# Two layers with attention, scan and experts: the experts' slots emptied in pieces, from zeros in memory, during the second batch

## The chip, the cores and the metric

The kernel runs on one core of a Trainium2 chip. The metric is device time in microseconds (us), as the median of several runs of the whole program. The core has five engines with a queue each: TensorE (PE, with its weight loads PEld), VectorE (DVE), ScalarE (ACT), GpSimd (POOL) and SyncE (SP). SP does nothing but issue transfers. POOL issues transfers too, the gathering and scattering ones among them. All transfers are carried out by 16 DMA engines.

## The reference

There are two layers over x of shape (4, 1024, 256), in float32. Each adds the product of a branch and a gate to x:

```python
xn = _layernorm(x)
s = attention_and_mlp(xn)            # layer 0: linear attention with cos and sin features
g = silu(rwkv_ffn(xn))
x = x + s * g
xn = _layernorm(x)
s = mamba(xn)                        # layer 1: a scan over time with 16 states
g = silu(two_experts(xn))            # layer 1: routed experts, this part is touched
x = x + s * g
```

The experts are routed. For every token a softmax over 8 experts is taken and the best two are picked. The first one works on the token; the second one works on the token plus half of the first one's output. The two outputs are weighted by their gate values, added to the token and normalised:

```python
topk_vals, topk_idx = top_k(softmax(x @ gate_W + gate_b), 2)
eo0 = expert[topk_idx[0]](x)
eo1 = expert[topk_idx[1]](x + 0.5 * eo0)
out = layernorm(x + topk_vals[0] * eo0 + topk_vals[1] * eo1)
```

## The kernel before, in words

The 4096 tokens are taken in 8 blocks of 512 (TB), two to a batch. Layer 0 goes batch by batch. For each batch there are eight key groups and eight query groups (the loop over `groups` in the kernel's main part). In one group, PE projects keys or queries (L729, L740), ACT and DVE take the sines (L762, L764, L765, L397), and PE multiplies them into kv or pa (L801, L832). Around these groups other work is dealt out in small steps from generators: `before_attention` (normalisation L506 to L522, transposes, projections), `after_attention` (the MLP with its weights fetched by L630 and L637, the second branch), and, as soon as a block is through layer 0, the scan of layer 1 (`decay` with the bcs load L946 on SP, `scan_step` with L1014, L1017 or L1023, L1032 and L1035).

When all blocks are through layer 0, the experts run beside the rest of the scan. Tokens are sorted by their expert through a table in memory. `slots[0]` has 5888 rows (NPAD, that is 23 tiles of 256) of 260 words for the first choice; `slots[1]` has rows of 516 words for the second choice. GpSimd scatters the tokens into their slots (L1272) and reads each tile of slots back with a plain transfer (L1291). Not every slot gets a token. An empty slot has to hold zeros and, in its last four words, row numbers that lie beyond the used part, so that what is computed for it is scattered where nobody reads. So the first 5888 rows of both tables are emptied before the scatters. The zeros come from `blank` and the four last words from `nowhere`, which is filled by POOL (L1125, L1127). The scatters are made to wait for the emptying through the lists `blanked`.

What sets the order of the work: the whole program is first written down in program order. At the end `arrange` replays it with assumed durations and one assumed queue for all transfers, and picks for PE, DVE and ACT one instruction after another: among those that are ready, the one with the lowest turn. A turn is the place in program order, moved for some names by a number of instructions (the table LATER). The order found is then fixed for these three engines. The queues of SP and POOL are not fixed by it.

```python
SIGNAL, LANDING, PER_BYTE = 60.0, 2000.0, 1 / 260
ENGINES = ("PE", "DVE", "Activation")
...
x.turn = k + LATER[behind].get(x.engine, {}).get(re.sub(r"_?[ab]?\d.*$", "", name), 0)
...
queue = max(queue, free[engine] + 300) + x.bytes * PER_BYTE
end = queue + LANDING - 300
```

On-chip tiles of one tag share a fixed number of buffers. `blank` is such a tile of the tag "w" in the pool work0, with five buffers, which also holds the x blocks of layer 0.

Of the kernel before, what the change touches and what calls it, by code (L numbers as in the profile page):

```python
# [15 lines left out]
F32 = mybir.dt.float32  # L16
U32 = mybir.dt.uint32
# [6 lines left out]
P = 128  # L24
# [17 lines left out]
ROW = 2 * D + 4  # L42
# [322 lines left out]
def kernel(  # L365
# [3 lines left out]
    nc = tc.nc  # L369
    const = ctx.enter_context(tc.tile_pool(name="const", bufs=1))  # L370
    dram = ctx.enter_context(tc.tile_pool(name="dram", bufs=1, space=DRAM))
# [17 lines left out]
    def col(name, i=0):  # L389
        return vec[:, COL[name] + i : COL[name] + i + 1]  # L390
# [10 lines left out]
    def accumulate(ps, pairs):  # L401
        for i, (lhs, rhs) in enumerate(pairs):
            nc.tensor.matmul(ps, lhs, rhs, start=i == 0, stop=i == len(pairs) - 1)  # L403
# [10 lines left out]
    def bank(name):  # L414
        return ps_bank.tile([P, TB], F32, name=name, tag="bank")
# [5 lines left out]
    work = l0.enter_context(tc.tile_pool(name="work0", bufs=5))  # L421

    def fetch_x(j):
        t = work.tile([P, NT, D], F32, name=f"x_{j}_{nc.next_id()}", tag="w")
        nc.gpsimd.dma_start(out=t, in_=tokens(x[j * TB : (j + 1) * TB, :]))
        return t
# [8 lines left out]
        out=bias_s, in_=rows_a.rearrange("a d -> (a d)").partition_broadcast(P)  # L435
# [62 lines left out]
    def normalize(pool, src, tag, twice=False):  # L498


        st = small.tile([P, NT, 6], F32, name=f"st_{tag}", tag="ln_st")
        bufs = 4 if twice else 2
        mv = pool.tile([P, NT, 2], F32, name=f"mv_{tag}", tag="ln_mv", bufs=bufs)
        rs = pool.tile([P, NT], F32, name=f"rs_{tag}", tag="ln_rs", bufs=bufs)
        for t in range(NT):
            nc.vector.bn_stats(st[:, t, :], src[:, t, :])  # L506
            nc.vector.bn_aggr(mv[:, t, :], st[:, t, :])
        nc.vector.tensor_scalar(rs, mv[:, :, 1], EPS, None, ALU.add)
        nc.gpsimd.tensor_tensor(rs, rs, mhalf, ALU.pow)
        if not twice:  # L510
            return mv, rs
        both = small.tile([P, NT], F32, name=f"rs2_{tag}", tag="ln_rs2")
        nc.vector.tensor_tensor(both, rs, rs, ALU.mult)
        nc.vector.tensor_tensor(both, both, mv[:, :, 1], ALU.mult)
        nc.vector.tensor_scalar(both, both, EPS, None, ALU.add)
        nc.gpsimd.tensor_tensor(both, both, mhalf, ALU.pow)
        nc.vector.tensor_tensor(both, both, rs, ALU.mult)
        return mv, rs, both

    def apply(dst, src, mv, rs):  # L520
        for t in range(NT):
            nc.vector.tensor_scalar(  # L522
                dst[:, t, :], src[:, t, :], mv[:, t, 0:1], rs[:, t : t + 1], ALU.subtract, ALU.mult
            )

    def transposed(src, c, tag):

        ps = bank(f"tr_{tag}")
        for t in range(NT):
            nc.tensor.transpose(ps[:, t * P : (t + 1) * P], src[:, t, c * P : (c + 1) * P], ident)  # L530
        return ps
# [4 lines left out]
    def bias(n, tiles=NT):  # L536

        return bias_s[:, n : n + 1, :].to_broadcast([P, tiles, D])

    def before_attention(b, s):  # L540

        j = b * (L // TB) + s
        tag = f"a{j}"
        xi = x_first if j == 0 else fetch_x(j)
        yield "N"
        mv, rs, both = normalize(keep, xi, tag, twice=True)
        kept[j] = (mv, rs)
        apply(xi, xi, mv, both)
        yield "N"
        x2t = work.tile([P, NC, TB], F32, name=f"x2t_{tag}", tag="w")  # L550
        for c in range(NC):
            ps = transposed(xi, c, f"{tag}{c}")
            nc.scalar.activation(
                x2t[:, c, :], ps, AF.Identity, bias=col("ln1_b", c), scale=col("ln1_g", c)
            )
        yield "N"
        qt = keep.tile([P, NC, TB], F32, name=f"qt_{tag}", tag="qt", bufs=2)
        kt = keep.tile([P, NC, TB], F32, name=f"kt_{tag}", tag="kt")

        v = keep.tile([P, NT, D + DH], F32, name=f"v_{tag}", tag="v")  # L560
        for dst, w, name in ((qt, wq_s, "bq"), (kt, wk_s, "bk")):
            for m in range(NC):
                ps = bank(f"p{name}_{tag}{m}")
                accumulate(ps, [(w[:, c, m * P : (m + 1) * P], x2t[:, c, :]) for c in range(NC)])
                nc.scalar.activation(dst[:, m, :], ps, AF.Identity, bias=col(name, m))
            if name == "bq":
                yield "K"
        nc.gpsimd.memset(v[:, :, D:], 0.0)
        for i in range(NT // 2):
            ps = bank(f"pv_{tag}{i}").rearrange("p (u d) -> p u d", u=2)  # L570
            for u in range(2):
                t = 2 * i + u
                accumulate(
                    ps[:, u, :],
                    [(x2t[:, c, t * P : (t + 1) * P], wv_s[:, c, :]) for c in range(NC)],
                )
            nc.vector.tensor_tensor(v[:, 2 * i : 2 * i + 2, :D], ps, bias(0, 2), ALU.add)
        keys[b, s] = (qt, kt, v)
# [513 lines left out]
    def beside(j, hf):  # L1092
# [23 lines left out]
    NPAD = NST * TS  # L1116
    slots = [
        dram.tile([NPAD, ROW - D], F32, name="slots0", tag="slots0"),
        dram.tile([2 * NPAD, ROW], F32, name="slots1", tag="slots1"),
    ]  # L1120
    fused = dram.tile([NB * L + NPAD, D], F32, name="fused", tag="fused")
    blank = work.tile([P, ROW - 4], F32, name="blank", tag="w")
    nc.gpsimd.memset(blank, 0.0)
    nowhere = w1p.tile([P, NPAD // P, 4], U32, name="nowhere", tag="nowhere")
    nc.gpsimd.memset(nowhere, 0)  # L1125
    for at_col, first in ((0, NPAD), (2, NB * L)):
# [1 line left out]
            nowhere[:, :, at_col], pattern=[[P, NPAD // P]], base=first, channel_multiplier=1  # L1128
        )
    blanked = ([], [])  # L1130
    for k, t in enumerate(slots):
        a = t[:NPAD, :].rearrange("(a p) d -> p a d", p=P)
        width = a.shape[2] - 4
        blanked[k].append(
            nc.sync.dma_start(
                out=a[:, :, :width],
                in_=blank[:, :width].unsqueeze(1).to_broadcast([P, NPAD // P, width]),
            )
        )
        blanked[k].append(nc.sync.dma_start(out=a[:, :, width:].bitcast(U32), in_=nowhere))  # L1140

    def needs(later, earlier):
        tc.add_manual_dep(
# [379 lines left out]
    def first_unit():  # L1523
        yield from prepare_block(0)
        yield from prepare_unit(0, 0)

    before.add(before_attention(0, 0))
    while before.force():
        pass
    for b in range(NB):  # L1530
        groups = [("k", b, s, t) for s in range(2) for t in range(NT)]
        groups += [("q", b, s, m, par) for s in range(2) for m in range(NC) for par in range(2)]
        for c, group in enumerate(groups):
            if c == 0:
                before.add(before_attention(b, 1))
            elif c == 4:
                while before.force():
                    pass
            elif c == 12 and b + 1 < NB:
                before.add(before_attention(b + 1, 0))  # L1540
            if before.wants == "K" and c >= 12:
                before.wants = "N"
            cycle(group, quota=(2, 3 if scans.ahead else 6, 2 if scans.ahead else 6, 0))
            for s in range(2):
                if len(at.get((b, s), ())) == NC:
                    after.add(after_attention(b, s, at.pop((b, s))))
            if 0 in ready and not blocks and not scans.side.todo:
                scans.side.add(first_unit())
                while not units:
                    scans.side.force()  # L1550
        while before.force():
            pass
# [87 lines left out]
```

## Time and profile before

| | |
|---|---|
| median of 3 runs | 2220.71 us (2216.21 to 2221.44) |
| the profiled execution, its own time | 2219.3 us |
| its span, from the first to the last instruction | 2217.6 us |
| granted TensorE clock, mean | 0.88 |
| busy share PE, DVE, ACT, POOL | 80%, 87%, 63%, 23% |
| slots from blank, first table | 5888 KB, 26.2 us from issue to landing |
| slots from blank, second table | 11776 KB, 48.9 us from issue to landing |
| slots from nowhere, both | 92 KB each, 36.8 us (median) |

The profile gives, for one execution, the busy time of each engine, the idle time ahead of each group of instructions with what ended it, and for every transfer the time from issue to landing. In the rows with 40 digits a digit is the busy share of one fortieth of the span (or of the window asked for), in tenths. A timeline shows the instructions of an engine in order, with start and duration. SPq and POOLq are the queues from which these engines issue; an issue that lasts long was held back. In 277 to 560 us DVE is busy 256.74 us and PE 235.08; in the same way every later stretch up to 2070 us has DVE above 90%, but for 1390 to 1480 us (62.87 of 90), in which the tokens are scattered.

### The profile page before, as it was taken

The page shows a single profiled execution, that of the slowest core. Times are in us where ns is not written, and L with a number is a line of the kernel's source. Part 1 is how long each engine was busy: PE and PEld are TensorE (multiplying, and loading weights), DVE is VectorE, ACT ScalarE, POOL GpSimd, SP SyncE. Part 2 cuts the span into 40 slices and gives each one's busy share as a digit, 9 for nine tenths or more (in the row PEclk, how much of TensorE's full clock was granted, in tenths as well). Part 3 has the DMA queues.
Part 4 walks back from the last instruction along what each step waited for, and adds up shares of the span by engine and source line. Part 5 has one row for each costly group of instructions (what it writes and reads, how often), then busy time and mean ns, then how long its engine had stood idle before and what let it go on. Part 6 is the DMA issues. An engine that isn't in the chain of part 4 may idle for free. (4 is left out here: it accounts for less than half of the span.)

```text
span 2217.6 us, 25392 instructions
## 1 busy us (share of the span) xinstructions
PE 1776.2 (80%) x9192; PEld 1232.7 (56%) x9192; DVE 1939.0 (87%) x2508; ACT 1389.7 (63%) x2039; POOL 501.2 (23%) x459
## 2 busy tenths in 40 slices
PE   6789679789987889969888777367988879899754
PEld 3335346444654545645456555256777658778643
DVE  4582669999999899889999999858998999989998
ACT  4664468797887788697875264334554555455584
POOL 1000100101100111000010110844544435445210
PEclk9789789789998989979998796588999989999877
DMA  9601123323332332323334354666777857877553
GB/s 274 170 19 48 57 87 103 107 68 95 83 108 85 115 86 78 105 75 107 114 89 136 117 159 128 164 200 202 227 243 222 240 200 247 280 230 224 190 191 103
DMA packets 145086, 320.22 MB, mean 144 GB/s; under 512 B 23344, under 2 KB 43952, under 8 KB 139072
## 3 DMA queue, kind: packets, MB, share of 16 engines
q1 hardware_dynamic: 110704, 170.02, 28.8%
q0 software_dynamic: 34256, 148.58, 19.3%
q8 instruction: 73, 1.20, 0.2%
q14 instruction: 53, 0.43, 0.1%
HBM read 256.86 MB, written 61.69 MB: 144 GB/s over the span
## 5 line engine op out<-in xcount | busy, mean ns | idle before, releaser
L496 ACT ACTIVATE da<-dt,neg_a 128x512 f32<-128x512 f32 x512 | 336.0, 715 | 157.1 <-PE y L1035 101.1
L1035 PE MATMUL y<-ident,da 128*128 128x128 f32 x2048 | 304.6, 298 | 126.8 <-DVE da L1032 120.3
L1035 PEld LDWEIGHTS y<-ident,da 128*128 128x128 f32 x2048 | 257.8, 154 | 193.3 <-DVE da L1032 95.8
L1032 DVE TENSOR_TENSOR da<-h,bcs 128x1024 f32<-128x1024 f32 x256 | 311.2, 1217 | 0.9
L1017 DVE TENSOR_TENSOR_SCAN h<-da,h 128x1024 f32<-128x1024 f32 x128 | 290.9, 2281 | 10.7 <-ACT da L496 8.8
L1014 DVE TENSOR_TENSOR h<-dtu,bcs 128x1024 f32<-128x1024 f32 x240 | 287.8, 1212 | 9.9 <-DMA bcs<-bcd 9.3
L1023 DVE TENSOR_TENSOR_SCAN h<-da,h_tail,h 128x512 f32<-128x512 f32 x224 | 277.2, 1268 | 8.8 <-ACT da L496 8.0
L403 PE MATMUL ph<-xst,we 128*128 128x256 f32 x736 | 178.9, 396 | 10.0 <-ACT xst L1309 9.3
L488 ACT ACT_TABLE_LOAD x134 | 171.9, 1283 | 3.2 <-PEq L1625 0.8
L403 PE MATMUL po<-we,ht 128*128 128x256 f32 x736 | 171.0, 385 | 1.1 <-ACT ht L1321 0.9
L403 PEld LDWEIGHTS ph<-xst,we 128*128 128x128 f32 x736 | 141.7, 198 | 34.6 <-ACT xst L1309 12.9
L403 PEld LDWEIGHTS po<-we,ht 128*128 128x128 f32 x736 | 139.6, 193 | 31.0 <-issue 6.6
L403 PE MATMUL ph_b<-x3t_b,w_b 128*128 128x512 f32 x256 | 119.8, 618 | 9.6 <-DVE fs_k L765 5.2
L403 PE MATMUL py_b<-w_b,ht_b 128*128 128x256 f32 x512 | 116.8, 385 | 4.7 <-ACT ht_b L643 1.7
L1321 ACT ACTIVATE ht<-ph,we 128x256 f32<-128x256 f32 x184 | 76.7, 470 | 65.0 <-PE ph L403 52.2
L403 PEld LDWEIGHTS py_b<-w_b,ht_b 128*128 128x128 f32 x512 | 97.4, 193 | 23.2 <-ACT ht_b L643 3.4
L801 PE MATMUL kv<-fs_k,v_a 128*32 128x256 f32 x1024 | 84.2, 475 | 29.6 <-ACT fs_k L496 29.6
L1309 ACT COPY xst<-pxs 128x512 f32<-128x512 f32 x46 | 26.9, 585 | 120.6 <-PE pxs L1305 120.6
L1272 POOL DMA_INDIRECT fused<-xs x46 | 86.4, 1878 | 44.5 <-DVE xs L1338 32.0
L1272 POOL DMA_INDIRECT slots<-xs x46 | 89.8, 1953 | 18.5 <-issue 10.1
L765 DVE SCALAR_TENSOR_TENSOR fs_k<-fs_k,fk 128x512 f32<-128x512 f32 x128 | 80.0, 678 | 15.7 <-ACT fs_k L764 15.7
L832 PE MATMUL pa<-fs_q,kvp 128*32 128x512 f32 x512 | 83.5, 675 | 12.5 <-ACT fs_q L496 12.5
(239 smaller groups left out, 3388.9 us busy)
## 6 DMA issues: line engine op xcount, KB each, us to landing
bcs<-bcd SPq DMA_DIRECT2D x240, 512.0 KB, 5.2
xs<-slots POOLq DMA_DIRECT2D x23, 516.0 KB, 4.9
x<-in_x_dram POOLq DMA_DIRECT2D x23, 512.0 KB, 5.2
slots<-blank SPq DMA_DIRECT2D x1, 11776.0 KB, 48.9
w_b<-in_w_dram POOLq DMA_DIRECT2D x16, 512.0 KB, 4.4
w_b<-in_w_dram POOLq DMA_DIRECT2D x32, 256.0 KB, 3.0
xs<-slots POOLq DMA_DIRECT2D x23, 260.0 KB, 3.9
slots<-blank SPq DMA_DIRECT2D x1, 5888.0 KB, 26.2
```

Of the source, the lines that this page charges most:

```text
L403: nc.tensor.matmul(ps, lhs, rhs, start=i == 0, stop=i == len(pairs) - 1)
L488: nc.scalar.preload_act_table_set({"E": "natural_log_exp_and_others", "S": "silu_and_others"}[which])
L496: in_turn(nc.scalar.activation(out, in_, func, **kw))
L765: nc.vector.scalar_tensor_tensor(t[:, 1, :], t[:, 0, :], -ROUND, ps[r], ALU.add, ALU.subtract)
L801: nc.tensor.matmul(kv[b][r // 2][32 * g : 32 * g + 32, r % 2, :, :], v[:, t, h * DH : (h + 2) * DH], f[:, :, m, par, :], start=(s, t, r % ...
L832: nc.tensor.matmul(pa[b, s][32 * r : 32 * r + 32, :], kvp[b][:, e, 4 * m + r, par, :], features(fs, r)[:, e, :], start=(par, e) == (0, 0), ...
L1014: nc.vector.tensor_tensor(h, dtu, bcs[:, 0:1, :].to_broadcast([P, UNIT, TB]), ALU.mult)
L1017: nc.vector.tensor_tensor_scan(flat, da.rearrange("p w t -> p (w t)"), flat, 0.0, ALU.mult, ALU.add)
L1023: nc.vector.tensor_tensor_scan(h[:, w, :], da[:, w, :], b[w], h_tail[:, c, n : n + 1], ALU.mult, ALU.add,)
L1032: nc.vector.tensor_tensor(da, h, bcs[:, 1:2, :].to_broadcast([P, UNIT, TB]), ALU.mult)
L1035: nc.tensor.matmul(y[:, t, w * P : (w + 1) * P], da[:, w, t * P : (t + 1) * P], ident, is_transpose=True, start=False, stop=(n, t % 2, w) ...
L1272: i = nc.gpsimd.indirect_dma_start(out=dst, out_offset=IndirectOffsetOnAxis(ap=index, axis=0), in_=src, in_offset=None)
```

## The change

The zeros are set in a tile of the pool work0 as before, but one transfer on SP then writes them to a tensor `blank` in memory, of 128 rows with 512 words. The four transfers that emptied the two tables at this place are gone. In their stead a generator `blank_slots` empties the tables in pieces: for each piece a transfer of zeros from memory to memory, and one of `nowhere` for the last four words, both on SP. A piece is `per` columns of 128 rows; NPAD // P is 46, so `per` is 7 and the pieces of a table begin at 0, 7, 14, 21, 28, 35 and 42. The generator is stepped once at the head of each of the sixteen groups of every batch but the first, until it is through.

```diff
-    blank = work.tile([P, ROW - 4], F32, name="blank", tag="w")
-    nc.gpsimd.memset(blank, 0.0)
+    zeros = work.tile([P, ROW - 4], F32, name="zeros", tag="w")
+    nc.gpsimd.memset(zeros, 0.0)
+    blank = dram.tile([P, ROW - 4], F32, name="blank", tag="blank")
+    nc.sync.dma_start(out=blank, in_=zeros)
...
-    for k, t in enumerate(slots):
-        a = t[:NPAD, :].rearrange("(a p) d -> p a d", p=P)
-        width = a.shape[2] - 4
-        blanked[k].append(
-            nc.sync.dma_start(
-                out=a[:, :, :width],
-                in_=blank[:, :width].unsqueeze(1).to_broadcast([P, NPAD // P, width]),
-            )
-        )
-        blanked[k].append(nc.sync.dma_start(out=a[:, :, width:].bitcast(U32), in_=nowhere))
+
+    def blank_slots():
+
+        per = NPAD // P // 6
+        for k, t in enumerate(slots):
+            width = t.shape[1] - 4
+            for c in range(0, NPAD // P, per):
+                n = min(per, NPAD // P - c)
+                a = t[c * P : (c + n) * P, :].rearrange("(a p) d -> p a d", p=P)
+                blanked[k].append(
+                    nc.sync.dma_start(
+                        out=a[:, :, :width],
+                        in_=blank[:, :width].unsqueeze(1).to_broadcast([P, n, width]),
+                    )
+                )
+                blanked[k].append(
+                    nc.sync.dma_start(
+                        out=a[:, :, width:].bitcast(U32), in_=nowhere[:, c : c + n, :]
+                    )
+                )
+                yield
...
+    blanking = blank_slots()
     before.add(before_attention(0, 0))
     while before.force():
         pass
...
         for c, group in enumerate(groups):
+            if b:
+                next(blanking, None)
             if c == 0:
                 before.add(before_attention(b, 1))
```

## The prediction

> **What bounds the kernel now.** I read the page first.
>
> ```profile
> span 2217.6 us, 25392 instructions
> PE 1776.2 (80%) x9192; PEld 1232.7 (56%) x9192; DVE 1939.0 (87%) x2508; ACT 1389.7 (63%) x2039; POOL 501.2 (23%) x459
> DMA  9601123323332332323334354666777857877553
> ```
>
> VectorE (DVE) is busy 87% of the span, so over the whole it is nearest to the bound. But each digit of the DMA row stands for 55 us, and the change concerns the 9 and the 6 at its left. Next, the timeline of SP, whose columns are start and duration in us:
>
> ```profile
> 13.72 2.95 SPq L375 DMA_DIRECT2D wout<-in_wout_t_dram  x1
> 16.79 0.89 SPq L1135 DMA_DIRECT2D slots<-blank  x1
> 18.46 16.38 SPq L1140 DMA_DIRECT2D slots<-nowhere  x1
> 34.90 12.44 SPq L1135 DMA_DIRECT2D slots<-blank  x1
> 47.38 25.71 SPq L1140 DMA_DIRECT2D slots<-nowhere  x1
> 251.33 0.36 SPq L857 DMA_DIRECT2D xt<-xt_d  x1
> ```
>
> The emptying follows the last weight. By the list of issues the second blank lands 48.9 us after 34.90, at 83.8; in 40 slices of 0 to 110 us the DMA share is 9 until about 85 us. SP then does nothing until 251.33. The chain of waits from 0 to 140 us shows who suffers. Compute waits for a transfer only three times, and only for the first loads: DVE 2.7 us and ACT 0.6 for vec, DVE 1.4 for x_first. Nothing waits for a transfer from 7 to 110 us. So the traffic to be moved away costs nothing where it is: **the expected gain of clearing the start is 0**.
>
> **Where the pieces will really go.** The change puts them into the second batch in program order. That sets an engine's order only where something holds it. The hand-made order covers PE, DVE and ACT; POOL and SP are left to the scheduler. POOL's timeline shows what it does:
>
> ```profile
> 3.49 0.93 POOL L630 DMA_DIRECT2D w_b<-in_w_dram  x1
> 7.42 1.04 POOL L509 TENSOR_TENSOR rs_a<-rs_a,mhalf 128x4 f32<-128x4 f32 x1 [3.00 <-DVE rs_a L508]
> ```
>
> L630 belongs to after_attention, written long after the first normalisation (L509), yet goes out first: a transfer with its buffer free and no input to wait for is drawn forward. A piece needs only the zeros in memory and nowhere, and SP is idle from 73 to 251 us. I expect all pieces at the start, just after the weights: moved in the source, hardly moved in time. I give this 0.89.
>
> **The sum, part by part.** *Pieces.* Each table has 5888 rows, 46 columns of 128; the step is 46//6 = 7, so a table gives seven pieces (six of seven columns and one of four): fourteen in all and 28 transfers, not twelve pieces. Data rows are 5888 of 1 KB and 5888 of 2 KB, 17.7 MB as before, and 11776 marks of 16 bytes as before. Added: one write of the zeros, 256 KB, behind wout (lands at 13.72 + 9.1 = 22.8), so pieces start near 24 us, not 17.
>
> *Transfer time.* No row shows a copy from memory to memory. From below: as before, 83.8 - 16.8 = 67 us, end near 91. From above: the Trainium skill, "DMA: Bandwidth & Descriptors", section "Where 436 GB/s comes from", gives HBM about 358 GB/s per core. That speaks against the change, as each byte is now also read from HBM: 35.3 MB / 0.358 = 99 us as an estimate. The marks come on top: in the slices, GB/s falls to about 10 twice, for some 8.5 us each, with the engines still busy, so 17 us; end near 24 + 116 = 140 us. The row at hand is 324 to 383 GB/s for SBUF to memory, already the rule's figure for one direction, so I take the middle, 115 us. What is late then? Two x loads issued at 109.95. Alone they land in 5.2 us (median), beside the weights one took 9.3. DVE first reads that x at 117.51; 109.95 + 9.3 = 119.3 is 1.8 us late. By the row the sum is 0, by the rule +1.8; I take 0.9.
>
> *Issue.* The four issues held SP 0.89 + 16.38 + 12.44 + 25.71 = 55.4 us. 28 cost 28 x 0.4 = 11 us free, or as long as the transfers last when held back, up to 116. The cover is SP's wait ahead of L857:
>
> ```profile
> SPq L857 <- DMA xt_d<-xg_b: 178.2, 1, 178.2
> SPq L1140 <- DMA wo<-in_wo_dram: 0.7, 1, 0.7
> ```
>
> Even 140 us leaves 111 of it. Without the cover, each us would delay xt and with it the first scan. The second line is a transfer waiting for the one eight places before it; with 28, about four pieces are in flight, at least 3.7 MB, some 10 us of traffic, so I count no hole.
>
> *Scatters.* Those of L1272 name 14 transfers instead of 2. They landed 1250 us earlier. A satisfied wait on POOL is 17 ns (EVENT_SEMAPHORE rows of L425): at most 14 x 17 = 0.24 us for each table, 0.5 in all, and this counts, as from 1390 to 1480 us POOL is busy 61 of 90. The work buffer comes free at 23 instead of 84 us; the next x after block 1's waits until 109.95 in any case: 0.
>
> *The planned order.* The planner replays one queue for all transfers and, in its books, put x of block 1 behind the first emptying (5.9 MB). The trace has that x landed at 11.04 + 9.3 = 20.3 us; yet its normalisation stands where the plan put it, behind the second key group. The timelines of DVE and ACT:
>
> ```profile
> 37.95 1.28 DVE L765 SCALAR_TENSOR_TENSOR fs_k<-fs_k,fk 128x512 f32<-128x512 f32 x2 [1.88 <-ACT fs_k L764]
> 39.16 1.29 DVE L397 TENSOR_SCALAR fs_k<-fs_k 128x1024 uint32<-128x1024 uint32 x2
> 40.36 0.74 DVE L506 BATCH_NORM_STATS2 st_a<-x 128x6 f32<-128x256 f32 x2
> ...
> 45.41 1.38 DVE L522 TENSOR_SCALAR x<-x,mv_a,rs_a 128x256 f32<-128x256 f32 x4
> ```
> ```profile
> 39.88 2.00 ACT L496 ACTIVATE fs_k<-fs_k 128x1024 f32<-128x1024 f32 x2 [1.38 <-DVE fs_k L397]
> 41.78 2.17 ACT L496 ACTIVATE fs_k<-fs_k,half_pi 128x1024 f32<-128x1024 f32 x2
> 47.49 1.45 ACT L553 ACTIVATE x2t_a<-tr_a,vec 128x512 f32<-128x512 f32 x2 [3.53 <-PE tr_a L530]
> ```
>
> Pieces that wait for the zeros in memory stand behind x in those books too, so the normalisation should move ahead of the group. Its ten DVE rows sum to 4.27 us; less the idle 1.88 before 37.95, the group is 2.4 us later (bounds 0 and 4.3). The sines end at 43.95 + 2.4 = 46.4, and x2t starts there instead of 47.49. The kv matmuls end 2.5 us after the sines now (46.44 to 43.95); ahead of the projections they end at 48.9, 0.6 later than the 48.32 at which these start now; behind them, x2t's lead of 1.1 stays. So -1.1 to +0.6, up to +2.5 if the gap is not filled; I take 0.
>
> *Numbering.* A LATER entry shifts an instruction by a count of instructions, and 28 new ones stand among those of the second batch. Some neighbours change places there and in what follows. No row prices this. Place: the second batch, 227 to 560 us, where DVE is busy 289.87 of 333.00 us, 43.1 idle. A better order can save a fraction of that idle time, a worse one add the like. I bound it by a quarter, 11 us either way, and take 0: neither direction follows from the profile.
>
> The sum on the profiled execution: 2219.3 (span 2217.6 and 1.7 around it) + 0 + 0.9 + 0.5 + 0 + 0 = 2220.7. The median of the runs shown is 1.4 above that execution: about **2222 us**.
>
> **The rivals.**
> - *A worse order (slower).* One mechanism: exchanged places make DVE wait in the second batch and after. Price 11 us, 2233. It decides from 6.7 us, when DVE's share from 227 on falls from 87.0% to 289.87/339.7 = 85.3%. For it: DVE is the fullest engine, so every wait there counts. Against: the counts shift by few places only.
> - *A better order (faster).* The same spread on the other side, 2222 - 11 = 2211. For it: the plan has x near its real landing. Against: as worked out, DVE and ACT are full from 28 to 48 us.
> - *The pieces do go out in the second batch.* A pair is 0.92 or 1.84 MB: 2.8 or 4.9 us at 330 or 375 GB/s plus 1.4 of marks, so 4.2 or 6.3; at the HBM rule 6.5 or 11.7. What stands behind is bcs. Its 256 steps run from 306.5 to 2186, 7.3 us each; a load issued two steps ahead has 14.7, needs 5.2, so 9.5 to spare. Cost 0 by the row, 7 x 2.2 = 15 by the rule. DVE waits 9.3 us for bcs today; I take that doubled: 2231.
>
> **How the numbers follow.** 0.3% is 6.7 us, about what a measurement of this kernel tells from no change. Likeliest, 0.45: pieces at the start, order as good, 2222 (own range 2214 to 2227). Worse order 0.25 (2233), better order 0.19 (2211), pieces in the second batch 0.11 (0.08 slower, 0.03 same). So faster 0.19, same 0.48, slower 0.33. The range takes in both order cases and a little beyond them: 2207 to 2240; about 0.1 is left out at each end.
>
> **What the profile after would show.** Right: SP issues blank near 17 us and 28 slots transfers from about 24, none after 150; L946 waits as now; st_a of block 1 stands ahead of L765 of the second key group; POOL's scatters start as close together as now. Wrong: slots transfers among the bcs ones between 227 and 560; x loads near 110 landing later than 10 us; DVE's share from 227 to 560 away from 87% by more than 1.7 points. A different order of PE, DVE and ACT throughout would make the prediction wrong at its weakest step, the numbering.

## The result, and the profile after

The changed kernel takes 2229.62 us (2224.49 to 2235.43, 10 runs) against 2222.18 (2216.21 to 2234.03, 10 runs) beside it: a ratio of **1.0033, interval 1.0018 to 1.0048**. Forecast were 2222, own range 2214 to 2227, and 2207 to 2240 with the other cases. The time lies inside the wide range, 7.6 us above the number, and just past the 0.3% that the prediction called no change, with an interval that reaches to both sides of it. Repeated on another occasion (22 runs) the changed kernel gave 2228.17, 1.0025 (1.0013 to 1.0037). So some 6 to 7 us have to be found.

The page of the changed kernel, its first lines, the granted TensorE clock and the DMA row:

```profile
span 2230.6 us, 25429 instructions
PE 1781.4 (80%) x9192; PEld 1236.7 (55%) x9192; DVE 1939.0 (87%) x2508; ACT 1390.1 (62%) x2039; POOL 503.4 (23%) x459
...
PEclk8779789789999989979898887579999989899877
DMA  8911123323333322223334463656677667877653
```

DVE does the same work to 0.1 us (1939.0), so what was added is idle time. The DMA row is as full at its left as before: no transfer has left the start. SP's timeline (start, duration) says it outright:

```profile
16.44 1.23 SPq L375 DMA_DIRECT2D wout<-in_wout_t_dram  x1
18.54 0.34 SPq L1125 DMA_DIRECT2D blank<-zeros  x1
19.25 5.30 SPq L1149 DMA_DIRECT2D slots<-nowhere  x4
25.15 14.35 SPq L1143 DMA_DIRECT2D slots<-blank  x5
...
103.57 2.66 SPq L1143 DMA_DIRECT2D slots<-blank  x1
106.27 1.53 SPq L1149 DMA_DIRECT2D slots<-nowhere  x1
250.88 0.37 SPq L857 DMA_DIRECT2D xt<-xt_d  x1
```

The pieces go out at 25, not in the second batch; four transfers of marks, which need no zeros, even pass ahead of them. (A mark is the four last words of an empty slot, from `nowhere`.) SP is through at 107.8, and xt of the first scan goes out at 250.88, 0.45 us earlier than before. SP's wait ahead of it, and DVE's for the x loaded while the last pieces were under way (list of waits, from 100 to 140 us for the second; us in total, times, longest):

```profile
SPq L857 <- DMA xt_d<-xg_b: 143.0, 1, 143.0
...
DVE st_a L506 <- DMA x<-in_x_dram: 2.2, 1, 2.2
```

The cover shrank from 178.2 to 143.0 and is still large. The x loads landed after 9.6 and 10.9 us, so one of them passed the 10 us that the prediction named as a sign of being wrong. DVE waited 2.2 us, of which the second batch shows nothing any more. In it DVE does the same share (before, then changed; columns of the table by stretch: length, then busy us and count of PE, PEld, DVE, ACT, POOL, then clock, DMA share, GB/s):

```profile
227.00:560.00 333.00, 265.64 (x1371) 155.15 (x1372) 289.87 (x420) 250.25 (x334) 33.96 (x41) 0.86 0.31 86
```
```profile
227.00:560.00 333.00, 265.89 (x1369) 155.02 (x1362) 290.59 (x420) 250.51 (x335) 33.56 (x42) 0.86 0.29 86
```

That is 290.59 us of DVE against 289.87 before, in the same 333 us. Matching each DVE instruction of one trace with the same one of the other gives the time by which it starts later. That difference is -0.4 us at 250, -0.7 at 580 and -1.4 at 1060: up to there the changed kernel is a little ahead. Then it is +3.2 at 1160, +4.7 at 1480, +3.1 at 1890, +9.8 at 1960 and +13.5 at the end. The pieces have been in memory for more than 900 us when the loss begins.

Which instructions stand where, engine by engine? DVE, ACT and POOL carry out the same sequence as before, but for the first 60 or so, in which the norm of block 1 moved ahead (its statistics at 31.90 us instead of 40.36); on PE two matmuls more changed places, some 650 matmuls into its 5990. An order that got worse is not there to be found. What does differ everywhere is one thing that no profile prints. The compiled program lists an address for every array in memory. The new array `blank`, 256 KB, takes the first place, and both tables, all activations, all coefficient arrays, the fused rows (the array into which the experts' results are scattered) and all branch arrays but one lie 262144 bytes further on.

### The profile page after: what moved, and what is told of

Same layout as the page of the kernel before. It is cut to its first block, busy times and chain, and to the rows that moved or that the text cites. A ratio compares the mean times of both kernels' runs of the same rounds, so it can differ in the third digit from the quotient of the medians.

```text
span 2230.6 us, 25429 instructions
## 1 busy us (share of the span) xinstructions
PE 1781.4 (80%) x9192; PEld 1236.7 (55%) x9192; DVE 1939.0 (87%) x2508; ACT 1390.1 (62%) x2039; POOL 503.4 (23%) x459
## 5 line engine op out<-in xcount | busy, mean ns | idle before, releaser
L832 PE MATMUL pa<-fs_q,kvp 128*32 128x512 f32 x512 | 85.3, 684 | 15.6 <-ACT fs_q L496 15.5
L1299 POOL DMA_INDIRECT we<-in_wcat_dram,wrow x46 | 76.1, 1655 | 67.9 <-ACT xst L1322 35.5
```

Source lines behind the costliest of these rows:

```text
L832: nc.tensor.matmul(pa[b, s][32 * r : 32 * r + 32, :], kvp[b][:, e, 4 * m + r, par, :], features(fs, r)[:, e, :], start=(par, e) == (0, 0), ...
```

## The experiments

Theories: **P**, the pieces or their traffic cost it; **O**, the changed early order, with the other use of buffers that follows from it; **M**, the place of the arrays in memory. All ratios below are to the kernel before, run beside it; it took 2221.07 us in 1 and 2, 2221.96 in 3, 2220.10 in 4 and 6, and 2221.18 beside the last run of 4. A ratio is not simply the quotient of the two medians and can differ from it by 0.001: the second kernel of 1 has 1.0010, its medians give 1.0020.

**1. Order and place, without the pieces.** Two kernels keep the two large transfers. The first adds a transfer of zeros into rows of the second table that are spare:

```diff
     nc.gpsimd.memset(blank, 0.0)
+    nc.sync.dma_start(out=slots[1][NPAD : NPAD + P, : ROW - 4], in_=blank)
```

> The kernel before, with one more transfer of 256 KB from its array of zeros into spare rows of the second table: the emptying stays two large transfers, no memory is added, but the order of the first 60 instructions of the other engines (the norm of block 1 ahead of the second key group) becomes that of the changed kernel. Theory P (the pieces as such cost the 7 us): 2222, as before. Theory M (the internal arrays lying 256 KB further on in memory cost it): 2222. Theory O (the changed order at the start costs it, by what it does to buffers later): 2229. My forecast of step 6 was a cost of 0 for this order, so 2222, within 4 us.

The second adds an array:

```diff
     nc.gpsimd.memset(blank, 0.0)
+    spare = dram.tile([P, ROW - 4], F32, name="spare", tag="spare")
+    nc.sync.dma_start(out=spare, in_=blank)
```

> The kernel before, with an unused array of 256 KB in memory into which the zeros are written once: the emptying stays two large transfers, the early order is that of the changed kernel, and every internal array in memory lies 256 KB further on, as in the changed kernel. P: 2222. M: 2229, and the reads of the tables and of the fused rows land about 8% later than before, as in the changed kernel. O: 2229. Together with the run that adds the transfer alone it tells M (this one slower, that one not) from O (both slower).

Measured: 2218.67, ratio **0.9984** (0.9972 to 0.9997), and 2225.56, ratio **1.0010** (0.9994 to 1.0027). So the early order shows no cost; with it the first kernel is even 3.5 us faster than before. (In that kernel the two tables have also exchanged places at the head of memory, as the second is written first; whether the gain is the order's or comes from this was not tried apart.) The order of theory O is out, unless a gain of this exchange hides its cost. The other use of buffers is not tried here, as both kernels keep the buffers of before. The second kernel is 0.0026, 5.8 us, above the first, and both have the same order of compute: M is left. (Its own interval still holds 1, so this run alone would not carry M.)

**2. The pieces, without the place.**

```diff
-    blank = dram.tile([P, ROW - 4], F32, name="blank", tag="blank")
-    nc.sync.dma_start(out=blank, in_=zeros)
+    blank = slots[1][:P, : ROW - 4]
+    first_rows = nc.sync.dma_start(out=blank, in_=zeros)
...
-    blanked = ([], [])
+    blanked = ([], [first_rows])
```

> The changed kernel without its 256 KB array in memory: the zeros are written into the first 128 rows of the second table and all other pieces are copied from there, so the pieces are as in the change and the internal arrays lie where they lay before. P: 2229. M: 2222. O: 2229.

The first piece of the second table leaves out the rows that serve as source. And the control:

> The changed kernel once more, on the same chip as the three others. P, M and O: 2229, 1.0018 to 1.0048 of the time before. If the 7 us came of the chip that the first comparison used: 2222, within 4 us of the kernel before. In its profile the waits of the expert stage for the fused rows (POOL, 42.8 us in the first profile of it, 27.4 before) should come again if they are the cause.

Measured: 2218.64, ratio **0.9977** (0.9963 to 0.9992), and 2228.17, ratio **1.0025** (1.0013 to 1.0037). The same pieces, the same buffers, the same order on PE, DVE, ACT and POOL, and 0.0048 (10.7 us) between them: P is out, and with it the other use of buffers. (Here too the tables have exchanged places; that no cost hides behind a gain of that exchange is seen only in 3.) Pieces against two large transfers, each time at the same places, is 0.9977 to 0.9984 and 1.0025 to 1.0010: -0.0007 and +0.0015, nothing that these runs resolve. The kernel with the pieces and without the array is faster than both kernels of this study.

**3. The place alone.** Unused rows behind the first table move everything else on. The queues of all five engines hold the same instructions in the same order as before, and all buffers on the chip lie where they lay; only addresses in memory differ:

```diff
-        dram.tile([NPAD, ROW - D], F32, name="slots0", tag="slots0"),
+        dram.tile([NPAD * (ROW - D) // 4 + 16384, 4], F32, name="slots0", tag="slots0")[: NPAD * (ROW - D) // 4, :]
+        .rearrange("(r k) c -> r (k c)", k=(ROW - D) // 4),
```

> The kernel before with 256 KB of unused rows behind the first table: no instruction is added, moved or removed on any engine, and every internal array but that table lies 256 KB further on in memory, as in the changed kernel. Theory M (the place in memory costs it): 2221 plus 4 to 9, so 2225 to 2230, and the scattered writes of the fused rows take over 300 us in sum (282 before, 306 and 317 in the two profiles of the changed kernel, 283 and 287 in the two kernels with arrays where they lay before). Theory N (the place is innocent, and what the slow kernels share is a further array in the compiled program or an accident of the order): 2221, sum 280 to 290.

Measured: 2229.70, ratio **1.0032** (1.0020 to 1.0044), the whole of the loss of the changed kernel with no instruction changed but for addresses. With 32768 and 4096 for 16384, and with the same edit made to the changed kernel:

> The same with 512 KB of unused rows. If M holds because addresses further on are slower, or because a shift breaks an alignment of the arrays: 2226 or more. If M holds in the form that each place is a draw (D): anything from 2214 to 2231, with no order among 64, 256 and 512 KB. N: 2221.

> The same with 64 KB of unused rows. M by distance: a quarter of what 256 KB cost, 2222 to 2223. M by broken alignment: as much as 256 KB, 2226. D: anything from 2214 to 2231. N: 2221.

> The changed kernel with 256 KB of unused rows behind the first table as well, so its other arrays lie 512 KB further on than before. M by distance or alignment: 2228 or more, and the same sign as the kernel before with 512 KB. D: it goes with the kernel before at 512 KB, since both share their places: within 4 us of it, whatever that is. P (the pieces as such cost 7 us): 2229.

Measured: 512 KB 2228.10, **1.0037** (1.0022 to 1.0051); 64 KB 2228.59, **1.0030** (1.0017 to 1.0042); the changed kernel at 512 KB 2228.61, **1.0027** (1.0016 to 1.0038). With all arrays but the first table at the same places, the changed kernel has 1.0025 and 1.0033 where the kernel before has 1.0032, and at 512 KB 1.0027 where it has 1.0037. So pieces, order and buffers together cost nothing that these runs resolve, and this does not lean on the exchanged tables. The loss does not grow with the distance: 64 KB cost what 512 KB cost. It is not the loss of an alignment to 64 KB or less, since all three shifts are multiples of that. Three places that are all equally bad speak against a free draw for each, too, which would have spread them.

**4. Which arrays.** The fused rows and what lies behind them, moved by enlarging the array ahead; the size of memory without any move of these; and everything between the tables and the fused rows, moved by 512 KB:

```diff
+    branch[4] = dram.tile([TB + 256, D], F32, name="branch4w", tag="branch4w")[:TB, :]
```

> The kernel before with 256 KB of unused rows behind one block's branch array (branch 4), which lies just ahead of the array of fused rows: the fused rows, two small arrays of scan coefficients and two branch arrays lie 256 KB further on, everything else (both tables, the blocks' activations, most coefficient arrays) where it lay. No instruction changes. If the place of the fused rows is what costs (F): 2228 to 2230, with the writes of the fused rows over 300 us in sum. If the place of the arrays ahead of it costs (A: activations and scan coefficients): 2222, and a sum of 280 to 290. If each costs a share: 2224 to 2226.

```diff
-    fused = dram.tile([NB * L + NPAD, D], F32, name="fused", tag="fused")
+    fused = dram.tile([NB * L + NPAD + 256, D], F32, name="fused", tag="fused")
```

> The kernel before with 256 unused rows (256 KB) at the end of the array of fused rows: the memory that the program takes grows as in the changed kernel, but only two branch arrays and one coefficient array move. If the total of memory costs, not the place (T): 2228 to 2230. If the place of the fused rows or of what lies ahead of them: 2222, within 3 us.

```diff
+    both = dram.tile([2 * TB, D], F32, name="both", tag="both")
+    x_mid[0], branch[4] = both[:TB, :], both[TB:, :]
```

> The complement of the run that moved the fused rows: in the kernel before, branch 4's array is taken out of its place and put behind the activations of block 0, so that all the blocks' activations, the branch arrays 0 to 3 and the coefficient arrays 0 to 5 lie 512 KB further on (the shift that gave 1.0037 when all moved), while both tables, the fused rows and what follows them lie where they lay. No instruction changes. If each part has its share (the fused rows' side gave 1.0015): 1.0015 to 1.0022, 2224 to 2226. If the fused rows' side is the whole cause and its 1.0015 was a low draw: 2221, within 3 us. If the activations and coefficients are the larger part: 2228.

Measured: fused rows moved 2224.82, **1.0015** (1.0001 to 1.0029); memory larger 2221.45, **1.0006** (0.9992 to 1.0021); activations and coefficients moved 2221.87, **1.0002** (0.9989 to 1.0016). For the total and for the activations these runs show no cost. The fused rows, with what lies behind them, explain about half of the 0.0032, with an interval that reaches from nothing to nearly all of it. The tables' place was not moved alone in one direction (in the two fast kernels of 1 and 2 both lie elsewhere than before, without harm), so whether the other half is theirs, or comes only with several arrays moved at once, stays open.

**5. What the traces show of it.** The list of issues, the scattered writes of the fused rows (count, median us to landing), for the pieces without the array, for the kernel before, and for the kernel before moved by 256 KB:

```profile
fused<-xs POOLq DMA_INDIRECT x46, 6.3
```
```profile
fused<-xs POOLq DMA_INDIRECT x46, 6.5
```
```profile
fused<-xs POOLq DMA_INDIRECT x46, 6.8
```

With the fused rows where they lay, the 46 writes take 282, 283, 287 and 297 us in sum (before, the two fast kernels, the larger memory); with the fused rows moved, 299 to 322 in nine profiles of eight kernels (the trace of the kernel with the activations moved has no landings of them). The medians part likewise, 6.3 to 6.5 and 6.7 to 7.2. Behind these writes stand POOL's reads of the next slots. From 1740 to 2080 us the list of waits has, for before, the changed kernel, its control, the pieces without the array, the kernel before moved by 256 KB, and the one with the larger memory:

```profile
POOL xs L1291 <- DMA fused<-xs: 27.4, 7, 5.6
```
```profile
POOL xs L1304 <- DMA fused<-xs: 42.8, 8, 7.9
```
```profile
POOL xs L1304 <- DMA fused<-xs: 39.7, 7, 9.1
```
```profile
POOL xs L1305 <- DMA fused<-xs: 27.5, 7, 6.4
```
```profile
POOL xs L1292 <- DMA fused<-xs: 31.1, 6, 8.9
```
```profile
POOL xs L1291 <- DMA fused<-xs: 33.1, 7, 8.5
```

The first four agree with the place of the fused rows as a cause. The last two do not: the slow kernel of the two, moved by 256 KB, waits no longer than the other. It is a tendency and no law: over all profiles the wait is 24 to 33 us with the fused rows in place and 25 to 52 with them moved, and the 52 belong to the second kernel of 1, whose ratio is 1.0010. So the landings show that the place is felt at these writes, but the loss of time is not accounted for by them.

The loss between 1060 and 1160 us looks different. Here are the pieces without the array first, then the control (columns as above):

```profile
1060.00:1080.00 20.00, 17.54 (x90) 11.24 (x90) 16.44 (x20) 17.62 (x25) 0.75 (x1) 1.00 0.34 96
1080.00:1100.00 20.00, 15.26 (x88) 8.50 (x84) 19.49 (x36) 18.32 (x28) 4.48 (x5) 0.91 0.47 132
...
1120.00:1140.00 20.00, 17.84 (x69) 7.54 (x68) 19.07 (x31) 16.00 (x22) 3.48 (x2) 0.91 0.24 78
```
```profile
1060.00:1080.00 20.00, 17.54 (x82) 10.60 (x81) 15.75 (x19) 16.11 (x23) 0.75 (x1) 0.91 0.33 105
1080.00:1100.00 20.00, 15.72 (x84) 8.97 (x82) 18.76 (x35) 17.73 (x26) 4.48 (x5) 0.83 0.33 108
...
1120.00:1140.00 20.00, 17.56 (x69) 8.27 (x69) 19.07 (x32) 15.52 (x21) 3.00 (x1) 0.83 0.22 56
```

In three of the five slices TensorE is granted a clock that is lower by 0.08 or 0.09. By groups of instructions from 1060 to 1165 us:

```profile
L403 PE MATMUL pi<-xt,win 128*128 128x512 f32 x16 | 8.8, 667 | 4.7 <-DVE fs_q L765 4.7
```
```profile
L403 PE MATMUL pi<-xt,win 128*128 128x512 f32 x16 | 11.1, 823 | 4.7 <-DVE fs_q L765 4.7
```

The same 16 matmuls take 2.3 us more. The start of DVE's instructions slips by 4.4 to 4.5 us here in every kernel with nearly all arrays moved by 256 or 512 KB, by 1.9 where only the fused rows and what follows them moved, and by nothing in the two fast kernels and the one with the larger memory. In all of them but the run of 6 some 1.6 to 1.7 us come back by 1230. This would make a good cause, but the last run of 4 speaks against it: with the activations moved the slip is there (+4.5 us) and the kernel is not slower (1.0002), while at 64 KB there is no slip and the kernel is (1.0030). So this dip of the clock comes with the place, but the loss cannot rest on it alone.

**6. The pieces where the source puts them.** Each is ordered behind the latest load of coefficients, and begins only when there is one (`lately` lists the transfers of L946; the fused rows lie where they lie in the changed kernel):

```diff
+                for piece in blanked[k][-2:]:
+                    tc.add_manual_dep(
+                        piece.ins, lately[-1].ins.name,
+                        mybir.DependencyInfo(
+                            mybir.DependencyClass.NoSync, mybir.DependencyReason.SCHED_ONLY
+                        ),
+                    )
...
-            if b:
+            if b and lately:
```

> The changed kernel with each of its pieces ordered behind the latest load of scan coefficients on SP's queue, so that they really go out during the second batch, one between two such loads; orders on the other engines as in the changed kernel, the fused rows where the changed kernel has them. My third rival put the cost of such pieces at about 10 us: 2228 + 10 = 2238, with the waits of the scans for their coefficients grown in the stretch from 250 to 560 us. If the transfers beside the scans are hidden: 2228, within 4 us.

Measured: 2230.03, **1.0049** (1.0033 to 1.0065), that is 0.0024 or 5.3 us above the control, with intervals that overlap a little. All pieces go out between 322 and 542 us. SP's timeline, and DVE's waits from 250 to 580 us, with the control's wait for the coefficients last:

```profile
325.99 13.06 SPq L947 DMA_DIRECT2D bcs<-bcd  x2
339.10 0.55 SPq L1145 DMA_DIRECT2D slots<-blank  x1
339.70 0.64 SPq L1151 DMA_DIRECT2D slots<-nowhere  x1
340.44 11.52 SPq L947 DMA_DIRECT2D bcs<-bcd  x2
```
```profile
DVE st_a L506 <- DMA x<-in_x_dram: 4.5, 1, 4.5
DVE h L1016 <- DMA bcs<-bcd: 4.0, 4, 1.8
```
```profile
DVE h L1014 <- DMA bcs<-bcd: 0.3, 1, 0.3
```

The control has no wait for x in this stretch. Its two x loads at 417 us land after 7.4 and 8.3 us, here after 11.4 and 12.1, and the coefficients take 7.6 us (median) instead of 5.0. DVE goes from 1.6 us ahead of before at 250 to 4.6 behind at 580, where the control goes from level to 1.2 ahead. The pieces are not all that differs: by the program's addresses both tables and the activations of the first two blocks lie elsewhere than in the control, and 3 has shown that the place alone can cost as much. The kernel before moved by 256 KB waits 1.1 us for the coefficients here and not for x (its x loads land after 7.8 and 8.8 us, its coefficients after 5.0), so in this stretch the pieces are the likely cause. That emptying in the second batch, the thing that the source describes, costs about 5 us more than emptying at the start is what the times say, with the place of these arrays not taken apart.

## Where the prediction held and where it missed, by its steps

- *Gain of clearing the start, 0.* Not put to the test by the change, which did not clear it. The run that did (6) is 1.6 us ahead of before at 250 us, the changed kernel 0.4 and its control 0.05: a gain of 1.2 to 1.5 us there at most, lost again in the second batch.
- *Pieces at the start.* Right: fourteen pieces and 28 transfers, between 25 and 108 us. The rule read off one POOL row, that a transfer with nothing to wait for is drawn forward, held for the marks as well.
- *Transfer time.* The end was taken at 115 us; the last blank landed at 118.8, at 111.2 in the control and at 106.9 without the array. From the first blank's issue that is 94, 87 and 83 us, between the bounds of 67 and 116 and near their middle. The prediction's 35.3 MB takes a KB as 1000 bytes; in the unit of the profile's GB/s it is 36.2 MB read and written (35.7 without the array), so 387 to 428 GB/s in both directions together, with the marks in it. The 358 GB/s of the Trainium skill ("DMA: Bandwidth & Descriptors", "Where 436 GB/s comes from") would ask for 101 us without the marks, as an estimate; so here the measurement is above the rule. That section forms the figure as half of the rate of a memory stack that two cores share, and this kernel runs on one core. The x loads: taken 0.9 us, DVE waited 2.2, gone by 250 us.
- *Issue and scatters, 0 and 0.5.* Right as far as seen: SP had 143 us to spare. The first eight scatters went out within 12.6 us (13.9 before and in the control).
- *The planned order, 0.* The move came as foreseen. DVE is 3.2 us ahead of before at 100 us, more than the 1.1 allowed for, but only 0.4 at 250. The first run of 1 shows no cost of it either.
- *Numbering, bounded by 11 us either way and called the weakest step.* It was not the weakest: two matmuls changed places. The rival built on it, the worse order, is refuted by its own mark: DVE's share from 227 to 560 us is 87.3%, not below 85.3%.
- **The step that failed** is the one that reads "Added: one write of the zeros, 256 KB". It priced the write and not the array. The array moves nearly all others, which by itself costs what the whole change cost (1.0032 against 1.0033 and 1.0025). The sum had no term for where arrays lie in memory, so no rival had one either; the range held the time by luck, only because another case, which did not come about, was wide. Why the new places are worse stays open.
- *Pieces in the second batch, 2231, so some 9 us.* Of the price taken, about half was there: 5.3 us by the times, with the reserve stated in 6. The bcs waits came as argued (4.0 us); the other wait is for an x load that lands late beside the pieces (4.5 us), which the rival did not name.

One reading of the profile after also fell. The jump of 6.7 us between 1890 and 1960 us in the changed kernel looks like its loss. But the two fast kernels have it against that same trace of before, +4.1 and +6.7 between 1890 and 1960, and end 7.6 and 9.6 us behind it, though their medians are lower. Their profiled executions took 2226.8 and 2228.4 us, 8 and 10 above their own medians. In the expert stage one profile is one draw, and a cause read from two single traces there needs the medians behind it. The changed kernel's own +13.5 us at the end is such a draw too: its control ends 9.8 us behind the same trace of before, and both are about 7 us slower by their medians.

## What to carry to other kernels

An added array in memory is a change to every array behind it: where a few tenths of a per cent are at stake, keep the addresses fixed when comparing, for instance with unused rows that take up the difference, and try the place alone before any story about queues. Before pricing a moved transfer, ask what holds it where the source puts it; without a dependency these went out at the start. A difference found by laying two traces side by side counts only if it comes again in kernels whose medians show it and is absent where they do not.

## What was not expected of the hardware

- Moving arrays in memory by 64, 256 or 512 KB, with every instruction the same, costs 6.7 to 8.2 us of 2222 (1.0030 to 1.0037), without order in the distance. Scattered writes to the moved fused rows land in 6.7 to 7.2 us instead of 6.3 to 6.5. Why these places are worse than the old one is not settled, and how much of the time these writes carry is not either.
- The place reaches the granted clock: from 1060 to 1140 us 0.91, 0.83, 0.83, 0.83 instead of 1.00, 0.91, 0.83, 0.91, and DVE is busy 90.81, 90.82 and 90.81 of the 100 us to 1160 in three kernels with moved arrays (the changed one, its control, the kernel before moved by 256 KB), 94.90 and 94.91 in two with them in place (before, and the pieces without the array). Moved by 64 KB it is 94.95, with the clock as in place. What leads from the place to the clock was not tried.
- Copies from memory to memory ran at 387 to 428 GB/s of reads and writes together, which is 193 to 214 counted once; before, zeros went from the on-chip tile to memory at 325 to 383 between the marks, with all transfers of that time counted.
